# Where the transfers that clear two scratch arrays are begun: spread over the slots, or three in a row behind the maxima

## The chip, the core and the metric

The kernel runs on one core of a Trainium2 chip. Its engines are TensorE (PE; its weight loads are shown apart as PEld), VectorE (DVE), ScalarE (ACT), GpSimd (POOL) and SyncE (SP), which computes nothing here and begins most of the transfers. The metric is the time of one execution on the device in microseconds, as the median of several runs. A profile is one execution with every instruction recorded; times inside it are counted from the start of its span.

## What is computed

The input `x` is 16 sequences of 256 tokens of 128 numbers. Cut to what matters:

```python
x = x + layernorm(attn0(layernorm(x)))            # causal, 16 heads of 8
h = layernorm(x)                                  # then a block of two layers on h
for l in range(2):
    h = h + attn(ln1(h), ...)                     # causal, 16 heads of 8
    g = ln2(h)
    h = h + (token_moe if l == 0 else seq_moe)(g) # 8 experts, the two best used
x = x + layernorm(h)
```

In the token layer every token goes through its own two experts of eight (128 to 512 to 128, GELU between); in the sequence layer a whole sequence goes through two experts, chosen from the mean of its tokens. So there are three attention stages of 16 sequences each, with a stage of experts behind the second and another behind the third.

## The kernel before

**Slots.** The order of all work is written out by hand. A `Plan` collects steps as (slot, phase, function); within a slot the phases are EARLY, MAIN and LATE, and equal ones keep the order in which they were put. Every engine gets its instructions in that order and works through them in order. A sequence's attention takes NT = 6 slots, and sequence i of the 48 starts at slot s0 = 6 i; `plan.shift` moves the third attention behind the token experts.

**Attention of one sequence** (`plan_sequence`). Scores are computed twice. `scores_max` (matmuls L276 and L299) runs LEAD = 10 slots ahead and DVE takes the maximum of every row (`mx`, L302). PE transposes the maxima (`transpose_max`, L493), ACT and DVE split them into a high and a low part (`mhi`, `mlo`), and SP sends these with two small transfers into rows 62 and 63 of `qk_rows` (L508), in slot 6 k + 3, phase EARLY. `scores_exp` (L276 and L320, from slot s0) reads them: a matmul then subtracts the maxima, and ACT takes the exponential (`pT`, L324). `weighted` (L339) multiplies by the values. Then `evict` and `compact` (L522, L523), `inverse` (L527, L528), `spread` (L534: `r`), `divide` (`y`, L541, on POOL) and `project_out` (`po`, L546). PSUM holds one bank pair `s1` for the maxima and one, `s2`, for the exponentials: the next maxima's matmuls wait until `mx` has been read.

**A pair of sequences** (`plan_pair`, once in 12 slots) is normed, transposed and projected; ACT and DVE write the result in a high and a low part (`hl`, L410 and L415), and SP copies it into `qk_rows` with eight transfers (`place`, L424) of 256 KB each: two late in slot s0 - 15, two early in the next, and four more two and three slots after the first. In the other six slots of the pair there are none of these.

**Behind the first attention** (`attention_0`, `after`): SP fetches `x` again as the residual (`xr`, L116), POOL adds it (`an`, L636), SP stores the sum (L637), and DVE and POOL norm it (`st_z`, `mv_z`, `rs_z`, `z`).

**The two scratch arrays.** The token experts work on tiles of 256 tokens of one expert. `x_rows` takes the tokens, scattered by POOL with indirect transfers (L883, after the layer's gate); its places that no token takes have to hold zeros. `y_rows` takes the results (L1176), from which `plan_combine` gathers two rows for each token (L756). Both are cleared beforehand from the tile `zeros`, with 88 transfers of 256 KB by SP: 68 for `x_rows`, 20 for `y_rows` (L1307). The n-th is put into slot 2 n.

**The token experts** (`plan_tokens`, in two parts of NA_T = 13 and 26 tiles). Each tile is fetched, transposed, taken through `plan_expert` (L1079, L1083, L1093), biased by DVE (`y_t`, L1172) and stored by POOL (L1176), five slots after its start. The first of the third attention's gathers (`plan_combine`, slot S_B + 2 NB_T + 2, LATE) fall among the last of these; NB_T is 14. The order between stores and gathers is set by hand: a list of the stores so far is handed to the first gather as its dependencies.

SP's transfers are given eight semaphores in turn, so that one also waits until the eighth before it has landed.

Of the kernel before, what the change touches and what calls it, by code (L numbers as in the profile page):

```python
# [18 lines left out]
B, T, D = 16, 256, 128  # L19
# [22 lines left out]
BA = 10  # L42
NB = B * T // TR
NTILE = 2 * B * T // TR + E - 1
NA_T = -(-(2 * BA * T - E * (TR - 1)) // TR)
NB_T = (2 * BA * T + E * (TR - 1)) // TR - NA_T
# [29 lines left out]
def sandwich_kernel(  # L76
# [13 lines left out]
    nc = tc.nc  # L90
# [100 lines left out]
    zeros = work.tile([P, 4 * D], F32, tag="w1", name="zeros", bufs=3)  # L191
# [68 lines left out]
    def transposed(srcs, tag, bank="m"):  # L260

        pt = ps_m.tile([P, 4, P], F32, tag=bank, name=f"pt_{tag}", bufs=2 if bank == "m" else 1)
        for i, src in enumerate(srcs):
            nc.tensor.transpose(pt[:, i], src, ident)
        return pt[:, 0 : len(srcs)].rearrange("p i t -> p (i t)")
# [82 lines left out]
    LEAD = 10  # L348
    NT = len(TILES)
    EARLY, MAIN, LATE = 0, 1, 2  # L350
# [270 lines left out]
    def attention_0(plan):  # L621
        def after(plan, s, b, po):
            st = {}

            def bias():
                st["x"] = load_x(b, "xr", 2)
                st["ao"] = work.tile([P, 2, D], F32, tag="ao", name=f"ao_{b}")
                bo = row[:, R_BOUT : R_BOUT + D].unsqueeze(1).to_broadcast([P, 2, D])
                nc.vector.tensor_tensor(st["ao"], po(), bo, ALU.add)

            def an():
                st["an"] = work.tile([P, 2, D], F32, tag="an", name=f"an_{b}")
                return st["an"]

            def residual():
                nc.gpsimd.tensor_tensor(st["an"], st["x"], st["an"], ALU.add)  # L636
                nc.sync.dma_start(x1_dram[b], st["an"])  # L637

            plan.put(s, bias)
            plan_norm(plan, s + 1, lambda: st["ao"], an, f"a{b}")  # L640
            plan.put(s + 3, residual)
            plan_norm(plan, s + 4, lambda: st["an"], lambda: z[b], f"z{b}")

        for g in range(B // 2):
            def source(k, g=g):
                return x0[2 * g + k]

            plan_pair(plan, 2 * g, 0, source, None, lambda dst, pt: nc.scalar.copy(dst, pt))
            for b in (2 * g, 2 * g + 1):
                if b + 4 < B:  # L650
                    def load(b=b):
                        x0[b + 4] = load_x(b + 4, "x0", 6)

                    plan.put(NT * 2 * g - 26 + 2 * (b % 2), load)
                plan_sequence(plan, b, 0, b, f"0_{b}", after)
# [92 lines left out]
    def plan_combine(plan, s, b, pace, adds):  # L748


        st = {}

        def gather(i):
            if i == 0:
                st["y"] = work.tile([P, 4, D], F32, tag="yg", name=f"yg_{b}")
            get = nc.gpsimd.indirect_dma_start(  # L756
                st["y"][:, i], None, y_rows,
                bass.IndirectOffsetOnAxis(ap=ix_y[:, 2 * b + i // 2, i % 2 : i % 2 + 1], axis=0),
            ).ins

            if i == 0 and b in (0, BA):
                for store in stores[: NA_T + NB_T] if b == 0 else stores[NA_T + NB_T :]:
                    tc.add_manual_dep(get, store.name, SYNC)
            apart_from(get, "y")

        def add(i):
            zt = z[b][:, i // 2]
            nc.vector.scalar_tensor_tensor(
                zt, st["y"][:, i], w_tok2[:, 2 * b + i // 2, i % 2 : i % 2 + 1], zt,
                ALU.mult, ALU.add,  # L770
            )

        for i in range(4):
            plan.put(s + i // pace, lambda i=i: gather(i))
            plan.put(adds[i // 2], lambda i=i: add(i))
# [34 lines left out]
    puts, stores, seen = [], [], [0]  # L810
# [15 lines left out]
    def apart_from(ins, group):  # L826

        tc.declare_no_dep(ins, group=group, reason="distinct rows")
        tc.add_to_no_dep_group(group, ins)
        nc.gpsimd.memset(apart, 0.0)  # L830
# [283 lines left out]
    def plan_tokens(plan, s, q):  # L1114

        x_blocks = x_rows.rearrange("(c i p) d -> c p i d", i=2, p=P)
        y_blocks = y_rows.rearrange("(c i p) d -> c p i d", i=2, p=P)
        spare = {}

        def room(m):  # L1120


            if m == 2:
                parts = work.tile([P, 8, 2, D], F32, tag="hl", name="x_hl", bufs=1)
                spare.update({2 + i: parts[:, i] for i in range(8)})
            if m == 10:
                parts = work.tile([P, 4, D], F32, tag="yg", name="x_yg")
                spare.update({m + i: parts[:, 2 * i : 2 * i + 2] for i in range(2)})
            if m == 12:
                spare[m] = work.tile([P, 4, D], F32, tag="xn", name="x_xn", bufs=1)[:, 0:2]  # L1130
            return spare.get(m)

        def unit(m):
            tag = f"t{q}_{m}"

            st = {}

            def fetch():
                if q:
                    load()  # L1140
                return nc.sync.value_load(ix_tile[q][0:1, m, 0:1], min_val=0, max_val=E - 1)

            def load():
                eng = nc.sync if q else nc.gpsimd
                c = eng.value_load(ix_tile[q][0:1, m, 1:2], min_val=0, max_val=BLOCKS - 1)
                st["xt"] = room(m) if q == 0 else None
                if st["xt"] is None:
                    st["xt"] = work.tile([P, 2, D], F32, tag="xr", name=f"xt_{tag}", bufs=2)
                get = eng.dma_start(st["xt"], x_blocks[bass.ds(c, 1)].squeeze(0)).ins
                for put in puts[seen[0] :]:  # L1150
                    tc.add_manual_dep(get, put.name, SYNC)
                seen[0] = len(puts)

            if q == 0:
                plan.put(s - 5 + m // 2, load, MAIN)

            def turn():

                st["pt"] = transposed(
                    [st["xt"][:, i] for i in range(2)], tag, "p" if q == 0 or m < NB_T else "m"  # L1160
                )

            def affine():
                st["h"] = work.tile([P, T], F32, tag="r", name=f"ht_{tag}")
                nc.scalar.activation(  # L1165
                    st["h"], st["pt"], AF.Identity,
                    bias=vec[:, C_LN2B : C_LN2B + 1], scale=vec[:, C_LN2W : C_LN2W + 1],
                )

            def done(po, b2):  # L1170
                y = work.tile([P, 2, D], F32, tag="ao", name=f"y_{tag}")
                nc.vector.tensor_tensor(y, po, b2.unsqueeze(1).to_broadcast([P, 2, D]), ALU.add)  # L1172
                st["y"] = y

            def store():
                store = nc.gpsimd.dma_start(y_blocks[NA_T * q + m], st["y"]).ins  # L1176
                stores.append(store)
                apart_from(store, "y")

            plan_expert(plan, s + 2 * m, tag, w_tok, fetch, lambda: st["h"], done)  # L1180
            plan.put(s + 2 * m + 5, store, EARLY)
            plan.put(s + 2 * m - 1, turn, MAIN)
            plan.put(s + 2 * m, affine, EARLY)

        for m in range(TILES_OF[q]):
            unit(m)
# [112 lines left out]
    plan = Plan()  # L1299
    start_steps(plan)  # L1300
    attention_0(plan)

    n = 0
    for t in (x_rows, y_rows):
        fill = t.rearrange("(c p r) d -> c p (r d)", p=P, r=4)
        for c in range(fill.shape[0]):
            plan.put(2 * n, lambda fill=fill, c=c: nc.sync.dma_start(fill[c], zeros))  # L1307
            n += 1
    layer_attention(plan, 0, B, finish_tok)

# [77 lines left out]
```

## Time and profile before

| | us |
|---|---|
| median of 3 runs (lowest, highest) | 1020.77 (1017.8, 1027.81) |
| the profiled execution, as timed | 1017.52 |
| its span in the profile | 1015.5 |
| PE busy | 923.1 (91%) |
| DVE, POOL, ACT busy | 674.6, 610.9, 568.0 |
| first and last clearing of `x_rows` begun at | 43.6, 350.7 |
| first and last clearing of `y_rows` begun at | 353.1, 440.8 |
| second attention ends, token experts run alone until about | 480, 640 |

The profiled execution is among the fast ones: 3.25 us under the median. A line of the waits is read as "who L-line <- what ended its idle time: us in total, times, longest us". In a timeline a line is: start, duration, engine and line, operation, output and inputs, count, and in brackets the idle time before it with what ended it. Idle time of an engine costs time only if the engine, or what waits for it, sets the end. For transfers begun by SP the profile has the time at which SP begins them, not that at which they land.

### The profile page before, as it was taken

To read this page: it belongs to the slowest core of one execution; us is meant where nothing else is said; L and a number is where in the kernel's file an instruction comes from. 1 tells how busy PE (TensorE), PEld (TensorE's weight loads), DVE (VectorE), ACT (ScalarE), POOL (GpSimd) and SP (SyncE) were. 2 spreads that over 40 slices of the span, in tenths; PEclk is the share of its full clock that TensorE was granted. 3 is DMA by queue.
4 is the path that set the end of the run, shared out by engine and by line. 5 is a ranking of instruction groups with operands and counts; after the bars stand their busy time and mean duration, and the time that the engine had idled before them with its cause. 6 is when DMAs were issued, how large, how long until landed. Compare 5 with 4: busy or idle time off the path is not lost. (4 is left out here: it accounts for less than half of the span.)

```text
span 1015.5 us, 29356 instructions
## 1 busy us (share of the span) xinstructions
PE 923.1 (91%) x11148; PEld 721.6 (71%) x11148; DVE 674.6 (66%) x1614; ACT 568.0 (56%) x903; POOL 610.9 (60%) x1028
## 2 busy tenths in 40 slices
PE   3799889999999999998889999889999999999996
PEld 1566666666667777775788898766676677689996
DVE  3668778888788888885433413468899988445433
ACT  3565556666566666565344555345666666754442
POOL 7114666667766477658675127658688643366655
PEclk8799999999999999998799999899999999999999
DMA  6657677777877765542656787935565556256773
GB/s 162 136 121 174 169 179 188 182 188 192 191 178 173 170 168 155 166 132 71 198 166 190 218 235 235 242 91 119 125 128 116 106 113 144 67 151 197 203 202 106
DMA packets 143900, 163.64 MB, mean 161 GB/s; under 512 B 26928, under 2 KB 109872, under 8 KB 143760
## 3 DMA queue, kind: packets, MB, share of 16 engines
q1 hardware_dynamic: 133920, 142.41, 57.2%
q0 software_dynamic: 7312, 17.18, 5.6%
q10 hardware_dynamic: 2528, 2.18, 1.0%
q8 instruction: 88, 1.44, 0.6%
q14 instruction: 52, 0.43, 0.1%
HBM read 65.38 MB, written 37.36 MB: 101 GB/s over the span
## 5 line engine op out<-in xcount | busy, mean ns | idle before, releaser
L302 DVE TENSOR_REDUCE mx<-s 128x4 f32<-128x1024 f32 (+1 forms) x288 | 350.6, 1218 | 94.2 <-PE s L299 89.8
L324 ACT ACTIVATE pT<-s 128x1024 f32<-128x1024 f32 x288 | 294.4, 1023 | 164.4 <-PE s L320 160.3
L276 PEld LDWEIGHTS <-pick 64*128 64x128 bf16 x2304 | 78.1, 95 | 144.6 <-issue 122.1
L299 PE MATMUL s<-qk_rows 62*128 62x128 f32 (+1 forms) x1536 | 160.4, 306 | 11.0 <-DMA qk_rows<-hl 11.0
L320 PE MATMUL s<-qk_rows 64*128 64x128 f32 (+1 forms) x1536 | 158.4, 305 | 9.1 <-DMA qk_rows<-mlo 9.1
L339 PE MATMUL av<-pT,va 128*32 128x256 f32 (+1 forms) x3072 | 156.3, 333 | 0.0
L299 PEld LDWEIGHTS s<-qk_rows 62*128 62x128 f32 x1536 | 114.2, 194 | 13.6 <-issue 11.6
L320 PEld LDWEIGHTS s<-qk_rows 64*128 64x128 f32 x1536 | 112.3, 193 | 12.9 <-DMA qk_rows<-mhi 11.6
L276 PE MATMUL s<-mask_q,pick 64*128 64x128 bf16 (+1 forms) x1152 | 95.0, 243 | 18.8 <-DVE mx L302 14.5
L1083 ACT ACTIVATE gs_t<-ph_t,w_t 128x256 f32<-128x256 f32 x156 | 65.3, 470 | 71.5 <-PE ph_t L1079 67.0
L276 PE MATMUL s<-mask_k,pick 64*128 64x128 bf16 (+1 forms) x1152 | 94.2, 242 | 11.6 <-ACT pT L324 9.4
L339 PEld LDWEIGHTS av<-pT,va 128*32 128x32 f32 x3072 | 79.7, 110 | 33.3 <-issue 1.1
L1083 ACT ACTIVATE gs_s<-ph_s,w_s 128x256 f32<-128x256 f32 x128 | 52.7, 470 | 59.4 <-issue 57.3
L1093 PE MATMUL pe_t<-w_t,gs_t 128*128 128x128 f32 x624 | 80.4, 284 | 2.1 <-DVE y_t L1172 2.1
L1079 PE MATMUL ph_t<-ht_t,w_t 128*128 128x256 f32 x312 | 79.2, 398 | 1.7 <-ACT ht_t L1165 1.2
L883 POOL DMA_INDIRECT x_rows<-zn,ix_tok x64 | 65.1, 1017 | 25.5 <-issue 14.8
L1093 PEld LDWEIGHTS pe_t<-w_t,gs_t 128*128 128x128 f32 x624 | 76.2, 199 | 3.5 <-DVE y_t L1172 2.6
L756 POOL DMA_INDIRECT yg<-y_rows,ix_y x64 | 64.3, 1004 | 13.0 <-issue 12.7
L1172 DVE TENSOR_TENSOR y_t<-pe_t,w_t 128x256 f32<-128x256 f32 x39 | 16.5, 422 | 81.0 <-PE pe_t L1093 72.7
L1079 PEld LDWEIGHTS ph_t<-ht_t,w_t 128*128 128x128 f32 x312 | 58.7, 199 | 10.9 <-DVE mx L302 1.6
L1176 POOL DMA_DIRECT2D y_rows<-y_t x39 | 28.9, 742 | 60.6 <-DVE y_t L1172 48.4
L1093 PE MATMUL pe_s<-w_s,gs_s 128*128 128x128 f32 x512 | 62.8, 276 | 0.6 <-issue 0.6
(205 smaller groups left out, 1505.8 us busy)
## 6 DMA issues: line engine op xcount, KB each, us to landing
qk_rows<-hl SPq DMA_DIRECT2D x188, 256.0 KB
x_rows<-zeros SPq DMA_DIRECT2D x68, 256.0 KB
w_t<-in_w_tok SPq DMA_DIRECT2D x39, 320.0 KB
w_s<-in_w_seq SPq DMA_DIRECT2D x32, 320.0 KB
w_t<-in_w_tok SPq DMA_DIRECT2D x39, 258.0 KB
w_s<-in_w_seq SPq DMA_DIRECT2D x32, 258.0 KB
y<-at SPq DMA_DIRECT2D x48, 128.0 KB
r<-inv SPq DMA_DIRECT2D x96, 64.0 KB
```

The lines of the kernel that those rows point to most:

```text
L276: nc.tensor.matmul(s[:, a, :, o + 64 * c : o + 64 * c + 64], pick[h, c], masks[m][h, 0:nj], start=(c == 0), stop=False, skip_group_check=True,
L299: nc.tensor.matmul(s[:, a, j], qs, ks, start=False, stop=(j == nj - 1), skip_group_check=True)
L302: nc.vector.tensor_reduce(mx[:, 0 if u is None else 1, :, j0 : j0 + nj], s, AX.X, ALU.max)
L320: nc.tensor.matmul(s[:, a, j], ks, qs, start=False, stop=(j == nj - 1), skip_group_check=True)
L324: nc.scalar.activation(pT, sc, AF.Exp, scale=SCALE)
L339: nc.tensor.matmul(o[:, P:] if u is None else o, v[:, i, 8 * par + 4 * a + jj % 4], p[:, a, j], start=(c not in first), stop=False, skip_g ...
L756: get = nc.gpsimd.indirect_dma_start(st["y"][:, i], None, y_rows, bass.IndirectOffsetOnAxis(ap=ix_y[:, 2 * b + i // 2, i % 2 : i % 2 + 1], ...
L883: put = nc.gpsimd.indirect_dma_start(x_rows, bass.IndirectOffsetOnAxis(ap=ix_tok[:, 4 * g + i, k : k + 1], axis=0), zns[2 * g + i // 2][:, ...
L1079: nc.tensor.matmul(p, w1[:, f * P : (f + 1) * P], h_of(), start=True, stop=True)
L1083: nc.scalar.activation(st["gs"][:, f], p, AF.Gelu, bias=b1[:, f : f + 1])
L1093: nc.tensor.matmul(po[:, i] if last is None else st["po"][i][:, 0], st["gs"][:, f, i * P : (i + 1) * P], st["w2"][0][:, f], start=(f == 0) ...
L1176: store = nc.gpsimd.dma_start(y_blocks[NA_T * q + m], st["y"]).ins
```

## The change

The clearing transfers are put into slots 3, 4 and 5 of every six, three in a row from the slot in which the maxima are sent, phase LATE, in place of every second slot. Beside that, the store of one tile of results (number 13 of the second part) goes one slot earlier, by which it comes ahead of the first two gathers, and two assertions state how many stores and scatters have been put in order at that time.

```diff
@@ plan_combine
             if i == 0 and b in (0, BA):
+                assert len(stores) >= (NA_T + NB_T if b == 0 else NTILE)
                 for store in stores[: NA_T + NB_T] if b == 0 else stores[NA_T + NB_T :]:
                     tc.add_manual_dep(get, store.name, SYNC)
@@ plan_tokens
                 get = eng.dma_start(st["xt"], x_blocks[bass.ds(c, 1)].squeeze(0)).ins
+                if m == 0:
+                    assert len(puts) == (4 * B if q else 4 * BA)
                 for put in puts[seen[0] :]:
@@
-            plan.put(s + 2 * m + 5, store, EARLY)
+            plan.put(s + 2 * m + (4 if q and m == NB_T - 1 else 5), store, EARLY)
@@ sandwich_kernel
     n = 0
     for t in (x_rows, y_rows):
         fill = t.rearrange("(c p r) d -> c p (r d)", p=P, r=4)
         for c in range(fill.shape[0]):
-            plan.put(2 * n, lambda fill=fill, c=c: nc.sync.dma_start(fill[c], zeros))
+            slot = NT * (n // 3) + (NT - LEAD + 1) % NT + n % 3
+            plan.put(slot, lambda fill=fill, c=c: nc.sync.dma_start(fill[c], zeros))
             n += 1
```

## Prediction

> **What bounds the kernel now.** I read the page's busy table first: PE is busy 923.1 of 1015.5 us, DVE 66%, ACT 56%, POOL 60%. The chain that ended last names almost nothing (PE 8%), so the end is set by PE's order and the gaps in it. The fills (the transfers that clear `x_rows` and `y_rows`) are issued from 43.6 to 440.8 us; what they can cost is idle time of PE in that stretch. So the second view is the waits between 40 and 310 us, one line a releaser (total us, times, longest us), from the answers for PE, POOL and DVE:
>
> ```profile
> PE s L320 <- DMA qk_rows<-mlo: 9.1, 10, 1.8
> ...
> PE po L546 <- POOL y L541: 2.2, 5, 0.5
> ...
> POOL an L636 <- DMA xr<-in_x: 28.4, 8, 4.2
> ...
> DVE st_z L237 <- POOL an L636: 12.7, 8, 2.2
> ```
>
> Ten times PE waits for the maxima rows (`mlo`, L508), 9.1 us in all: that is what the change addresses. The third line matters as much: eight times POOL waits for `xr`, the residual input that SP fetches behind the `hl` rows. The third view is the timeline of one of these stretches, SP's queue first (start, us, line, operation):
>
> ```profile
> 204.73 2.62 SPq L424 DMA_DIRECT2D qk_rows<-hl  x4
> 207.45 0.60 SPq L528 DMA_DIRECT2D inv<-sums  x1
> 208.10 0.95 SPq L1307 DMA_DIRECT2D x_rows<-zeros  x1
> 209.15 2.82 SPq L424 DMA_DIRECT2D qk_rows<-hl  x4
> 212.01 1.01 SPq L116 DMA_DIRECT2D xr<-in_x  x1
> ...
> 218.15 0.34 SPq L1307 DMA_DIRECT2D x_rows<-zeros  x1
> 219.06 0.57 SPq L508 DMA_DIRECT2D qk_rows<-mhi  x1
> 219.73 0.54 SPq L508 DMA_DIRECT2D qk_rows<-mlo  x1
> ```
>
> Eight `hl` transfers of 256 KB come in a burst once per pair of sequences (12 slots, about 27 us). The windows show it (columns: stretch, PE, PEld, DVE, ACT, POOL, clock, DMA share, GB/s):
>
> ```profile
> 206.00:211.00 5.00, 4.88 (x85) 4.05 (x84) 3.96 (x9) 2.83 (x5) 4.16 (x7) 1.00 1.10 209
> 211.00:212.50 1.50, 1.50 (x28) 0.79 (x26) 1.22 (x2) 1.00 (x2) 0.00 (x0) 1.00 1.10 314
> 212.50:217.00 4.50, 4.35 (x74) 3.33 (x73) 4.14 (x12) 3.52 (x6) 2.52 (x4) 1.00 1.15 197
> ```
>
> The DMA engines are full from 206 to 217 us and `hl` runs at about 200 GB/s. What is queued at 212 waits until 217. POOL, DVE and PE then show what follows from that, in the same stretch:
>
> ```profile
> 219.40 0.73 POOL L636 TENSOR_TENSOR an<-xr,an 128x256 f32<-128x256 f32 x1 [3.28 <-DMA xr<-in_x]
> ...
> 222.78 0.73 POOL L541 TENSOR_TENSOR y<-y,r 128x256 f32<-128x256 f32 x1
> ```
>
> ```profile
> 220.16 0.29 DVE L237 BATCH_NORM_STATS2 st_z<-an 128x6 f32<-128x128 f32 x1 [1.32 <-POOL an L636]
> ...
> 221.23 1.16 DVE L302 TENSOR_REDUCE mx<-s 128x8 f32<-128x1024 f32 x1
> ```
>
> ```profile
> 221.84 0.66 PE L320 MATMUL s<-qk_rows 64*128 64x128 f32 x8 [0.61 <-DMA qk_rows<-mlo]
> 222.45 0.29 PE L276 MATMUL s<-mask_q,pick 64*128 64x128 bf16 x4
> ...
> 223.56 0.71 PE L546 MATMUL po<-wvo_sb,y 128*128 128x128 f32 x4 [0.53 <-POOL y L541]
> ```
>
> `xr`, issued at 212.01, lets POOL start `an` at 219.40. From there POOL works without a gap to the end of `y` at 223.51, and PE's `po` starts 0.05 us later. DVE, held by `an`, ends `mx` at 222.39, and PE's L276 at 222.45 needs that bank. So the wait for the maxima (0.61 us) lies under a second chain, **xr, an, y or mx, PE**, which ends at the same moment. The engine that looks off the path is on it.
>
> **The change, part by part.**
>
> *The fills, order.* No instruction is added or removed; PE, ACT and DVE keep their order. Before, fill n is begun at slot 2n; after, at slots 3, 4 and 5 of every six, the maxima being sent early in slot 3. In the built program the burst becomes hl hl F hl hl inv F hl hl F hl hl xr, where it was hl x4, inv, F, hl x4, xr, with one fill ahead of it (served before 204 us, when the DMA was idle) and two behind `xr`. (In the last bursts, planned by `layer_attention`, the first of the three stands ahead of the first `hl`; the count is the same.) No bytes are added, but **two more fills stand between the first `hl` and `xr`**.
>
> *Cost of a fill in the burst.* Upper end: 262,144 bytes at some 345 GB/s, the rate of the fullest half microseconds while a fill is served, 0.75 us. Lower end: the burst moves 8 x 262 KB of `hl` in the 11.0 us from 206 to 217; at 197 GB/s that alone takes 10.6, so the one fill in it took 0.4. I take 0.55, between the two, since both are of the same burst: two fills 1.1 us (0.8 to 1.5).
> The Trainium skill's page "DMA: Bandwidth & Descriptors", section "Anatomy of one DMA — SWDGE (gpsimd) path", prices a transfer at about 2.0 us plus its bytes over 436 GB/s. By it `xr` (128 KB, issued at 212.0) would land by about 214.3, before POOL has finished the instruction ahead of `an` (at 216.11), and two fills issued earlier would cost nothing. The row says 7.4 us from issue to `an`: the fit is for one transfer alone, on the other queue, and here the queue is the price. I follow the row; with the page's bytes term a fill would be 0.60 us, two 1.2.
>
> *What PE pays.* `xr` lands 1.1 later, `an` and so `y` end 1.1 later. For the six stretches at 169, 197, 224, 250, 277 and 305 us `po` follows `y` within 0.1 us: 6 x 1.1 = 6.6. At 142 `y` ends at 142.71 and `po` starts at 142.84: 1.0. At 114 `y` ends at 113.48 and `po` starts at 113.90, so 0.7. Sum **+8.3 us** (5.5 to 11.5).
>
> *The maxima.* A transfer of SP also waits for the eighth before it. Before, `mlo` is issued at 219.73, behind `mhi` and a fill that waited for the seventh `hl` to land (218.1). After, the eighth before `mlo` is that seventh `hl` (in the stretches at 113 and 142 the eighth one), itself two fills later: 218.1 + 1.1 = 219.2. The maxima come about 0.5 us earlier, not more: the fill that left their front now stands in front of what they wait for. Under the xr chain this gives PE nothing in eight places. It counts at 84.20 (wait of 0.62, no `xr` there, `y` ended 2.6 before `po`): -0.4. The wait at 42.68 (1.65) has no fill ahead of it and stays. If the xr chain were not there, the most to be had is 9.1 - 1.65 = 7.4.
>
> *First maxima of the next pair.* PE needs the first four `hl` at 212.60; they now land one fill later (0.55). The trace shows no wait there; the slack lies between 0 and about 1.7 us (fourth `hl` issued at 206.74 and its bytes through by about 211). A wait of up to 0.55 falls ahead of the 1.1 + 1.1 us that PE idles later in the stretch, and is taken out of it: 0 (at most 8 x 0.55 = 4.4 if nothing absorbs it).
>
> *After 310 us* there is no `xr`, no wait for maxima, and `hl` issued from 338.18 is first used at 347.37, with its first four transfers through by about 344.5: 0; up to 0.5 in each of 7 bursts if that cover is thinner. The fill that ends `x_rows` moves two slots (4.6 us), to about 355; POOL's first scatter is at 359.0: 0, at most 1 us once. `y_rows` is filled 180 us before its use: 0. In the other half of each pair the DMA is lightly loaded: 0.
>
> *The store of tile 13 of the second part* (`NB_T - 1`) moves up one slot, ahead of the first two gathers of `plan_combine`, on POOL:
>
> ```profile
> 613.68 0.76 POOL L1176 DMA_DIRECT2D y_rows<-y_t  x1 [0.31 <-DVE y_t L1172]
> ...
> 614.74 0.99 POOL L756 DMA_INDIRECT yg<-y_rows,ix_y  x1 [0.23 <-issue]
> ```
>
> Before, two gathers (610.96 and 612.30) fill the time in which POOL would wait for `y_t`; after, POOL idles from 610.7 to 613.68, the store goes, and all four gathers of z[0] follow from 614.74. Everything behind is 2 x 1.28 = 2.6 us late. DVE's additions (620.77) wait for the fourth gather: 618.54 + 3.5 (median landing) = 622.0. POOL's `rs_i` (623.66) comes at 626.2, DVE's `xn` (624.79) at 627.3, and behind `xn` on DVE stands `y_t`, which frees PE's bank for the matmul at 625.91: now about 628.3. **+2.3 us**; ends 0.5 (POOL catches up) and 4.
> Does the gather also wait until the store has landed (3.4 us, median of that row)? The same page, "Two DMAs through the same engine are not ordered", says that only the completion semaphore orders them, which would put the gather at 617.1 and the sum 2.4 higher. The trace has gathers 0.26 us behind a store (609.94, 610.96), and in the changed program's list the first gather has no wait on that store's lane: I take none.
>
> **Sum.** 8.3 - 0.4 + 2.3 = +10.2 us. The profiled execution took 1017.52 (span 1015.5): 1027.7. The median of the runs shown is 1020.77, 3.25 above it, from which it would be 1031.0. I give 1029, between them. Own range 1023 to 1037.
>
> **Rivals.**
> *A, the maxima decide (faster).* If the two fills do not delay `xr` (they overlap with `hl`[...]: for it speaks the 0.4 end above), the 7.4 us of waits for maxima go, less what `y` and `mx` still hold; with the store's 2.3 against it, 1017.5 - 7.4 + 2.3 = 1012. It decides once a fill in the burst costs less than some 0.1 us. Against it: the DMA share is 1.10 to 1.15 in the burst, and `y` ends 0.05 before `po`.
> *B, no visible change.* The delay of `xr` and the gain of the maxima cancel, or later slack gives it back, and the store costs 0 to 3: 1018 to 1023, say 1020.
> *C, more is lost.* A fill costs its full 0.75, the first maxima wait as well, or the gather waits for the store: 11.5 + 4 + 2 = 1035.
>
> **How the numbers follow.** Forecast 0.50, A 0.14, B 0.24, C 0.12. About 1% (10 us) is what a measurement of this kernel can tell from no change. The forecast lies right at it: half of it counts as slower. Slower by over 1%: 0.26 + 0.11 and, since what I have costed at nothing can only add, 0.07 more: 0.44. Faster by over 1%: the lower half of A, 0.08. Within: 0.48. The range leaves out most of A and the end of C: 1015 to 1037.
>
> **What would show it.** Right: POOL's wait for `xr` grows from 28.4 by about 9 us over eight times; PE's wait for `mlo` falls to about 4 or less; PE's waits for `y` (L546) and for `mx` (L276) grow by about 8 together; between 610 and 635 us PE has about 2.3 us more idle time. Wrong: POOL's wait for `xr` stays at 28, or PE's waits for `mlo` go and nothing takes their place.

## The result, and the profile after

The changed kernel takes 1028.6 us (median of 13 runs, 1022.45 to 1038.1) against 1020.77 (13 runs, 1014.89 to 1027.81) for the kernel before: **1.0082 times, 95% interval 1.0058 to 1.0106**, or 5.9 to 10.8 us more. The ratios, and the mean clocks of runs below, leave out runs that took over 1.5% longer than the fastest of their kernel. The forecast of 1029 is met to half a microsecond. That is partly luck. From the median of before, the forecast's own sum of 10.2 us leads to 1031.0; it was set 2 us lower, between two bases, and the fills cost less than the sum said. The profiled execution took 1028.54 (span 1026.6), 11.0 more than the one before: near the 10.2, but with a loss of clock in it that the sum had no term for.

First the waits between 40 and 320 us in the kernel after (total us, times, longest us), the stretch in which fills and `xr` meet:

```profile
POOL an L636 <- DMA xr<-in_x: 35.6, 8, 5.1
DVE st_z L237 <- POOL an L636: 14.9, 8, 3.1
...
PE s L276 <- DVE mx L302: 8.7, 17, 1.5
...
PE po L546 <- POOL y L541: 4.0, 8, 0.5
PE s L299 <- DMA qk_rows<-hl: 3.9, 5, 1.0
PE s L320 <- DMA qk_rows<-mlo: 3.4, 3, 1.5
```

The wait for the maxima rows (`mlo`) fell from 9.1 to 3.4 us. In its place stand POOL's wait for `xr` (28.4 to 35.6), DVE's for `an` (12.7 to 14.9), and on PE the waits for `mx` (1.8 to 8.7) and `y` (2.2 to 4.0). One line is new: the first maxima wait for `hl` (3.9 us, five times). The cure of one wait is paid for in another, as forecast. The timeline of the stretch that the prediction showed (start, us, line, operation, idle time before it), SP first:

```profile
209.40 1.28 SPq L424 DMA_DIRECT2D qk_rows<-hl  x2
210.73 0.61 SPq L1312 DMA_DIRECT2D x_rows<-zeros  x1
...
213.68 0.84 SPq L1312 DMA_DIRECT2D x_rows<-zeros  x1
214.62 2.10 SPq L424 DMA_DIRECT2D qk_rows<-hl  x2
216.77 0.61 SPq L1312 DMA_DIRECT2D x_rows<-zeros  x1
217.42 1.22 SPq L424 DMA_DIRECT2D qk_rows<-hl  x2
218.68 0.97 SPq L116 DMA_DIRECT2D xr<-in_x  x1
```

```profile
224.51 0.73 POOL L636 TENSOR_TENSOR an<-xr,an 128x256 f32<-128x256 f32 x1 [3.73 <-DMA xr<-in_x]
...
227.90 0.73 POOL L541 TENSOR_TENSOR y<-y,r 128x256 f32<-128x256 f32 x1
```

```profile
227.57 0.29 PE L276 MATMUL s<-mask_q,pick 64*128 64x128 bf16 x4 [0.25 <-DVE mx L302]
...
228.68 0.71 PE L546 MATMUL po<-wvo_sb,y 128*128 128x128 f32 x4 [0.53 <-POOL y L541]
```

Three fills stand ahead of `xr`, POOL starts `an` 15.11 us after the burst's first `hl` (224.51 - 209.40), and `po` follows the end of `y` (228.63) by 0.05 us. No wait for `mlo` is left in this stretch. Before, the same distance was 219.40 - 204.73 = 14.67. So the two fills cost 0.44 in this stretch of this pair of executions, not the 1.1 of the sum.

The store of tile 13 did what was forecast. The matmul of PE that needs the bank freed by `y_t`, in the kernel after:

```profile
637.29 3.52 PE L1094 MATMUL pe_t<-w_t,gs_t 128*128 128x128 f32 x16 [2.28 <-DVE y_t L1175]
```

Before, no matmul waits for `y_t` there; the forecast was 2.3.

PE's projections (`po`, L546) are good milestones, 48 in each execution. Their times after less those before are: -0.45 at 85 us, +0.8 at 114, +1.8 at 143, **+3.6 at 156, +4.4 at 170**, +4.7 at 197, +5.1 at 224, +6.1 at 250, +7.3 at 277, +7.8 at 305, +9.3 at 318, then +9.0 to +9.3 from 344 to 482, and +10.7 to +11.0 from 723 on. The loss ends with the first attention, as forecast. But it doesn't come in equal steps of 1.1. At 156 and 318 us it jumps, where no `xr` is waited for. For the first jump the windows tell why (stretch, busy us of PE, PEld, DVE, ACT, POOL, granted clock, DMA share, GB/s). Before, from 85 to 155 us:

```profile
85.00:155.00 70.00, 64.52 (x956) 46.68 (x955) 56.40 (x114) 40.87 (x53) 43.12 (x69) 0.98 0.71 176
```

and after:

```profile
85.00:155.00 70.00, 64.74 (x888) 45.62 (x887) 52.87 (x107) 38.08 (x50) 40.72 (x64) 0.90 0.62 159
```

The granted TensorE clock was 0.90 instead of 0.98 in these 70 us. PE looks as busy as before and does 7% fewer matmuls. The prediction has no term for that. At 310 to 320 us, ahead of the second jump, 1.75 us of full clock are lost, and PE waits once for 1.8 us until ACT has written `pT`.

### The profile page after: what moved, and what is told of

It reads as the page before. It is cut to its first block, busy times and chain, and to the rows that moved or that the text cites. A ratio compares the mean times of both kernels' runs of the same rounds, so it can differ in the third digit from the quotient of the medians.

```text
span 1026.6 us, 29367 instructions
## 1 busy us (share of the span) xinstructions
PE 926.0 (90%) x11148; PEld 722.9 (70%) x11148; DVE 675.6 (66%) x1614; ACT 569.1 (55%) x903; POOL 613.2 (60%) x1028
## 5 line engine op out<-in xcount | busy, mean ns | idle before, releaser
L299 PE MATMUL s<-qk_rows 62*128 62x128 f32 (+1 forms) x1536 | 161.1, 307 | 14.9 <-DMA qk_rows<-hl 14.9
L339 PE MATMUL av<-pT,va 128*32 128x256 f32 (+1 forms) x3072 | 158.9, 337 | 0.0
L299 PEld LDWEIGHTS s<-qk_rows 62*128 62x128 f32 x1536 | 114.9, 195 | 19.2 <-issue 17.3
L276 PE MATMUL s<-mask_k,pick 64*128 64x128 bf16 (+1 forms) x1152 | 94.2, 242 | 12.0 <-ACT pT L324 10.7
L1175 DVE TENSOR_TENSOR y_t<-pe_t,w_t 128x256 f32<-128x256 f32 x39 | 16.5, 423 | 78.3 <-PE pe_t L1094 69.9
```

What stands on the lines that cost most here:

```text
L276: nc.tensor.matmul(s[:, a, :, o + 64 * c : o + 64 * c + 64], pick[h, c], masks[m][h, 0:nj], start=(c == 0), stop=False, skip_group_check=True,
L299: nc.tensor.matmul(s[:, a, j], qs, ks, start=False, stop=(j == nj - 1), skip_group_check=True)
L339: nc.tensor.matmul(o[:, P:] if u is None else o, v[:, i, 8 * par + 4 * a + jj % 4], p[:, a, j], start=(c not in first), stop=False, skip_g ...
```

## The experiments

The theories, as the expectations name them. **T1**: two more fills ahead of `xr` delay `an`, and with it `y`, `mx` and PE. **T2**: the late `hl` transfers, and the first maxima that wait for them (L299), carry the loss. **T3**: the store's wait is absorbed before the end. **T4**: only how many fills fall into the busy stretch counts. **Gate theory**: stalls that follow each other closely make the granted clock drop to half for some 3.4 us, and this is a part of every loss.

The runs were made on other chips than the first result. There the kernel before takes 1060 to 1068 us: the first 370 us are as fast as on the first chip (the projection at 358.76 comes at 357.50 in store_only, whose order is that of before up to there), the excess lies behind, where the change moves only the one store. So each ratio is against the kernel before on the same chip. The table also gives the time between the projections that stand at 85 and 359 us in the profile before, and the full clock lost between them: the sum over 5 us windows of 5 x (1 - granted clock).

| kernel | time against before (95%) | us from projection to projection | clock lost, us | the same at equal clock |
|---|---|---|---|---|
| before | 1 | 273.3 | 3.4 | 270.9 |
| before_again | | 279.1 | 12.0 | 270.6 |
| store_only | 1.0014 (0.9989 to 1.0039) | 273.3 | 3.4 | 270.8 |
| after | 1.0082 (1.0058 to 1.0106) | 282.8 | 8.4 | 276.8 |
| after_again | 1.0117 (1.0076 to 1.0157) | 286.8 | 15.4 | 275.9 |
| fills_only | 1.0040 (1.0013 to 1.0067) | 278.6 | 4.7 | 275.3 |
| fills_445 | 1.0103 (1.0070 to 1.0136) | 286.1 | 11.9 | 277.7 |
| fills_heavy | 1.0318 (1.0275 to 1.0361) | 309.1 | 30.7 | 287.3 |
| heavy_warm | 1.0345 (1.0303 to 1.0387) | 305.5 | 20.6 | 290.9 |
| fills_012 | 0.9883 (0.9827 to 0.9938) | 274.2 | 6.9 | 269.3 |
| fills_light | 0.9958 (0.9929 to 0.9987) | 272.1 | 5.1 | 268.5 |
| before_xr | 0.9983 (0.9957 to 1.0009) | 274.9 | 10.3 | 267.6 |
| fills_xr | 0.9883 (0.9843 to 0.9924) | 264.8 | 0.0 | 264.8 |
| light_xr | **0.9853** (0.9812 to 0.9893) | 259.8 | 0.0 | 259.8 |

The last column takes off 0.71 us for each us of clock lost. That slope is fitted to six executions: three with the fills of before (before, before_again, store_only) and three with those of after (after, after_again, fills_only), a level for each group and one slope for both. It is a fit to few points, and for fills_heavy and heavy_warm it is carried far beyond them.

**The two parts alone** (store_only, fills_only).

```diff
-            plan.put(s + 2 * m + 5, store, EARLY)
+            plan.put(s + 2 * m + (4 if q and m == NB_T - 1 else 5), store, EARLY)
```

> Before, with only the store of tile 13's tokens moved one gather place earlier (ahead of the first two gathers of the combine), the fills as in before. T1 and T2 (both treat the store as a separate step): the store begins its wait before the first two gathers, both gathers and so rs_i, xn and y_t come about 2.3 us later, a matmul of pe_t waits about 2.3 us for y_t, and the end comes 2.0 to 2.6 us later: about +2.3 us. Rival T3 (the wait is absorbed again before the end of the kernel): 0 to +0.5 us.

By time the store is worth -1.2 to +4.1 us, which doesn't tell 2.3 from nothing. The row does. The first fence is store_only, the second fills_only, where the store is at its old place:

```profile
650.69 2.64 PE L1093 MATMUL pe_t<-w_t,gs_t 128*128 128x128 f32 x16 [2.70 <-DVE y_t L1172]
```

```profile
650.41 2.05 PE L1093 MATMUL pe_t<-w_t,gs_t 128*128 128x128 f32 x16 [0.55 <-DVE y_t L1174]
```

The wait is 2.70 us with the store moved and 0.55 without: some 2.1 us go with the store. On the first chip PE's projections are 8.3 and 9.1 us late ahead of it (494 and 508 us) and 10.7 behind it (723 us), so 1.6 to 2.5 more. The rows speak against T3; by time it stays open.

```diff
-            plan.put(2 * n, lambda fill=fill, c=c: nc.sync.dma_start(fill[c], zeros))
+            slot = NT * (n // 3) + (NT - LEAD + 1) % NT + n % 3
+            plan.put(slot, lambda fill=fill, c=c: nc.sync.dma_start(fill[c], zeros))
```

> The fills as in after (slots 3, 4 and 5 of every six), the store of tile 13 at its place of before. T1 and T2: the whole loss of the fills' region, about +9 us less the 0.4 that comes back later, so +6 to +9 us against before by the chain, about +6 by the medians (after is +7.8 by its median, less 2.3 for the store). The wait for y_t in front of pe_t is back at its value of before. If the store carried the loss in another way than by that wait, this run is within 2 us of before.

+4.2 us (1.4 to 7.1): the fills are the larger part, but they cost less than the 8.3 of the sum, and less than the 6 to 9 expected here.

**xr taken out of the burst** (before_xr: with the fills of before; fills_xr: with those of after).

```diff
@@ attention_0, after
+            def residual_load():
+                st["x"] = load_x(b, "xr", 2)
+
+            plan.put(s - NT, residual_load)
             def bias():
-                st["x"] = load_x(b, "xr", 2)
```

> Before, with the fetch of xr issued six slots earlier, ahead of the burst of maxima rather than in it. T1 (xr behind the burst sets when an, st_z, mx and y come): POOL's an no longer waits for xr, PE's waits for y and mx fall to those of slots outside the burst; 1 to 4 us below before, since the wait for mlo at L320 remains. T2 (the late maxima transfers hl are what delay PE; xr is slack): within 1 us of before.

> The fills as in after, the store as in before, and xr fetched six slots earlier, so that three fills still stand in the burst but none ahead of xr. T1 (the two further fills cost what they delay xr by): the loss of the fills goes, 0 to 5 us below before, POOL's wait for xr about 0; the first maxima's waits at L299 (3.9 us in five places in after) remain or grow a little. T2 (the late hl transfers and what follows them carry the loss): +4 to +8 us against before, with the waits at L299 as large as in after or larger.

fills_xr is 12.4 us faster than before (8.1 to 16.7): with `xr` out of the way the three fills in the burst cost nothing. T2, which asked for +4 to +8, falls; T1 has the sign, but its gain of 0 to 5 us was too small. 8.5 us of the gain lie in the stretch of the table, 6.0 at equal clock. before_xr gains less: POOL waits no longer for `xr`, and yet only 1.8 us are gained (between a gain of 4.6 and a loss of 0.9). That is within T1's 1 to 4, but the interval doesn't rule out T2's "within 1 us". PE's waits for the maxima from 40 to 320 us in before_xr:

```profile
PE s L320 <- DMA qk_rows<-mlo: 7.8, 9, 1.5
```

Of PE's 9.1 us of waits for the maxima rows 7.8 are left. The fills of before stand ahead of these, and they end where the chain of `xr` ended. Of two chains that end together, taking one away gives little.

**Where the fills stand** (fills_445: slots 4, 4, 5 of six, the first four `hl` ahead of them; fills_012: slots 0, 1, 2; fills_light: slots 3 to 7 of twelve, none in the burst; light_xr: the same with the early `xr`). Only the line of the slot differs:

```diff
+            slot = NT * (n // 3) + (4, 4, 5)[n % 3]                     # fills_445
+            slot = NT * (n // 3 + 1) + n % 3                            # fills_012
+            slot = 2 * NT * (n // 6) + (3, 3, 4, 5, 6, 7)[n % 6]        # fills_light, light_xr
```

> The fills three in a row as in after, but begun half a slot to a slot later (slots 4, 4, 5 of every six, each behind the maxima of its slot), so that in the burst the first four hl transfers go out ahead of all fills, and all three fills still go ahead of xr; the store as in before. T1 (what counts is that two more fills stand ahead of xr): as with the fills alone, +3 to +7 us against before, the waits for xr at 33 to 36 us in the stretch 40 to 320, the waits for hl at L299 down from 5.2 us to under 2. T2 (the late first maxima, hl at L299, carry the loss): the waits for hl go and with them most of the loss, -1 to +2 us.

The waits for `hl` are gone, and the kernel is slower than with the fills alone. The lines are PE's and POOL's waits from 40 to 320 us in fills_445:

```profile
PE s L276 <- ACT pT L324: 10.9, 12, 2.0
PE s L276 <- DVE mx L302: 9.2, 17, 1.2
...
PE s L299 <- DMA qk_rows<-hl: 0.4, 1, 0.4
```

```profile
POOL an L636 <- DMA xr<-in_x: 35.2, 8, 5.6
```

T2 falls a second time. T1 has the sign and the wait for `xr`, but its +3 to +7 is too small against 7.4 to 14.5: in the 300 us of the table 7.3 us more of clock were lost than in fills_only (5.2 by the slope), and 2.4 us more at equal clock. For these the waits show a path that no theory had: PE's wait for `pT` doubled, from 5.2 us in fills_only to 10.9. The tile `hl` exists only once (`bufs=1` in the code), so ACT can write the next `hl` (L410), and behind it `pT`, only when the eight transfers have read the last one. What delays them delays ACT; fills_heavy below shows it most clearly.

> The fills three in a row in slots 0, 1 and 2 of every six: none of them ahead of xr in the burst, but three around and behind it, where before has one or two, and so ahead of mhi and mlo; the store as in before. T1 (xr's place in the queue): xr lands about 0.5 us sooner than in before, so POOL's waits for xr fall from 28 us to about 24, while mlo comes later and PE's waits for it at L320 rise from 9 us to 12 to 16: the sum is 0 to +4 us against before. Rival T4 (only how many fills fall into the busy stretch counts, not which transfer they delay): as with the fills alone, +3 to +7 us, with the waits for xr no shorter than in before.

The waits for `xr` fell to 24.5 us as T1 said, so T4 falls. PE's waits for `mlo` stayed at 9.8 us where 12 to 16 were expected. The time is 1.2% lower than before, below either range. In the 300 us of the table only 1.5 of that is found at equal clock; where the rest comes from is open. Behind its projection at 375 us the profiled execution of fills_012 takes 680 us; those of before_again, store_only, before_xr and fills_only, also on other chips than the first, take between 681 and 691 there.

> All six fills of a pair of sequences in its light half (slots 3 to 7 of every twelve), none in the burst's slots 9 to 12; the store as in before. T1: xr waits for no fill, mhi and mlo neither: POOL's waits for xr fall from 28 us to 22 to 25, PE's waits for mlo and mhi from 9 and 12 us to under 4 each: -3 to -9 us against before. T2 says the same sign by the hl transfers, but only -1 to -3 us, since in before they are hardly waited for.

4.5 us faster (1.4 to 7.5): right in sign and size. The waits for `mlo` and `mhi` fell to 1.5 and 1.8 us, those for `xr` only to 26.8, since `xr` still stands behind eight `hl`. (The profiled execution, whose waits these are, took 1066.32 us, 8 more than the median of this kernel.)

> The fills in the light half as in the run beside it, and xr fetched six slots earlier, ahead of the burst. T1 (xr and then mlo are what is waited for in the burst): no wait for xr is left, mlo and mhi wait for no fill: -10 to -15 us against before, at most 3 us better than the fills as in after with the early xr (which gave -12.4), since that had only the waits for hl at L299 left. Gate theory (stalls of 2 to 3 us one after the other make the granted clock drop to half for a window of some 3.4 us, and this is a part of every loss): the mean granted clock of the runs is 0.955 or more, against 0.947 in before, and the stretch from 80 to 320 us shows at most one stretch below 0.9. T2: within 3 us of the fills in the light half alone.

15.6 us faster (11.4 to 20), the best of all kernels here and a little more than the 10 to 15 expected. Neither chain is left, and each alone had given only 1.8 and 4.5. The first of its windows (the third column from the end is the granted clock):

```profile
85.00:155.00 70.00, 66.83 (x1009) 48.21 (x1006) 58.69 (x121) 43.59 (x56) 46.00 (x73) 1.00 0.82 189
```

The clock is full here and in the windows that follow up to 320 us. The mean clock of its runs is 0.954 at the median against 0.948, a hair under the 0.955 expected.

**What the clock is worth** (the two kernels unchanged, once more).

> The kernel after, once more, beside another execution of the kernel before. Between about 70 and 373 us the first profiles differ by 9.5 us (place of the projection at 85 against that at 372), and the granted clock cost after 8.6 us of full clock there against 3.4 in before. Gate theory (short stalls in a row make the clock drop to half for some 3.4 us, in windows that fall differently in each execution): the differences in these 300 us change from one pair of executions to the next with the lost clock, by about 0.6 us for each us lost, and what is left without it is 5 to 7 us in both pairs. Rival (the clock is only a mark of the waits): the difference stays 9 to 10 us whatever the lost clock. Over the whole kernel: +5 to +9 us, since the fills alone gave +4.2 and the store 1.5 by time and about 2.2 by its wait for y_t.

> The kernel before, once more, as the other half of the pair: waits for xr at 28 to 29 us and for mlo at about 9 us in the stretch 40 to 320, as in its first profile; one to three windows of half clock between 70 and 375 us, not at the same places.

By time the kernel after is 12.5 us slower in this pair (8.1 to 16.8), above the 5 to 9 expected but for the edge. The strongest row is that of the kernel before against itself. Its second profile, from 85 to 210 us:

```profile
85.00:155.00 70.00, 64.26 (x884) 46.06 (x884) 53.16 (x109) 38.25 (x49) 39.39 (x63) 0.90 0.67 165
155.00:210.00 55.00, 51.90 (x721) 36.76 (x714) 41.28 (x82) 30.50 (x40) 33.11 (x52) 0.91 0.72 171
```

The waits are those of the first profile (27.9 us for `xr`, 8.8 for `mlo`), the instructions the same, and the same 300 us take 5.8 us longer with 8.6 us more of clock lost, in four places where one to three were expected. One instruction shows it too. `po` of the fifth sequence, at half clock in after, and at full clock in fills_only, which has the same order up to there:

```profile
144.66 1.22 PE L546 MATMUL po<-wvo_sb,y 128*128 128x128 f32 x4 [0.19 <-POOL y L541]
```

```profile
143.91 0.71 PE L546 MATMUL po<-wvo_sb,y 128*128 128x128 f32 x4 [0.53 <-POOL y L541]
```

This is the jump of +1.8 between 143 and 156 us: fills_only loses nothing there. The first pair (after less before) differs by 9.5 us with 5.0 us more of clock lost, the second by 7.7 with 3.4. Taking off 0.71 a microsecond leaves 5.9 and 5.3, within the 5 to 7 expected, where the rival had the difference stay at 9 to 10. A third pair, fills_only less store_only, differs by 5.3 with 1.3 more: 4.4 are left. So the difference does move with the clock lost; three pairs don't give the size of what is left to better than a microsecond. Over 52 whole runs of before on one chip, too, the time goes up by 0.45 us for each us of clock lost (correlation 0.80).

The Trainium skill's page "TensorE: Matmul & The Clock Gate", section "Part 1: The HAM clock gate (the "warmup" mystery)", says that an idle window of about 3.4 us halves the clock, and that these windows run freely and don't start with the kernel. The traces agree in the length: a drop costs about 1.7 us of full clock (1.75 at 110 to 120 us in before) or twice that (3.4 at 140 to 150 us in after), which is 3.4 or 6.8 us at half. They agree in that the same program drops at other places in another execution. They don't show the idle window: no single wait of PE from 40 to 320 us is longer than 2.8 us in any run here, and from 140 to 144 us in after, ahead of and at the start of a drop, PE was busy in 1.71 of the 4 us. That PE's waits trip it is seen here only as company: this drop comes amid waits of 0.85 us (for `mlo`, until 141.60) and 1.28 us (for `mx`, until 143.54).

**More of the cause** (fills_heavy: all six fills ahead of `xr`; heavy_warm: with extra matmuls of zero weights).

```diff
+            slot = 2 * NT * (n // 6) + (9, 10, 10, 10, 11, 11)[n % 6]
```

> All six fills of a pair in slots 9 to 11 of every twelve, so that six instead of one stand ahead of xr in the burst (five more than before, where after has two more); the store as in before. T1 with the forecast's price (0.55 us a fill, 8 bursts that count): 5 x 0.55 x 8 = +22 us, the longest wait for xr 6.5 to 8 us. T1 with the price of the profiles (two fills moved POOL's an by 0.44 us in the stretch at 210 us, so 0.22 a fill): +9 us, and 2 to 5 more by the clock: +11 to +14, the longest wait for xr about 5.5. T2 (first maxima): the waits for hl at L299 grow from 5.2 to 15 us or more.

+34.7 us by the medians (29 to 39 by the interval), more than any theory had. `an` starts 17.65 us after the first `hl` on average, against 15.0 in before and 15.8 in after; the longest wait for `xr`, 6.6 us, is as T1 with the forecast's price had it. At equal clock five fills cost 287.3 - 270.8 = 16.5 us in the 300 us, 0.41 for each fill and stretch; the clock lost, 30.7 us against 3.4, is worth 19 if the slope holds so far out. T2 falls once more: the waits for `hl` at L299 are 0.5 us. But most of what PE newly waits for isn't T1's chain either. PE's waits for `y` and `mx` from 40 to 320 us are 10.8 us (4.0 in before), those for `pT` 19.5 (4.4 in before), one of 1.8 to 2.8 us in each of eight bursts. ACT and then PE, at 208 us:

```profile
208.36 0.69 ACT L410 ACTIVATE hl<-pp,vec 128x512 fp32r<-128x512 f32 x1 [3.17 <-DMA r<-inv]
```

```profile
210.01 0.40 PE L276 MATMUL s<-mask_k,pick 64*128 64x256 bf16 x4 [2.02 <-ACT pT L324]
```

This is the path of the single `hl` tile. ACT starts 0.23 us before POOL's `an` (208.59), since `xr` stands right behind the last `hl`. (The trace infers the releaser, and names `r`; the matmul that ACT needs was done at 206.) In after this path is hardly longer than in before (5.7 us against 4.4), so that the chain of `xr` is what the change lengthened. No run here gives `hl` a second tile.

> All six fills in slots 9 to 11 of every twelve, as in the run with 1.0318, and in the eighth slot-11 step of each pair of the first layer (ahead of PE's longest stall, 2.0 us in the stretch at 208 us) the twelve matmuls of `av` once more with zero weights, which add nothing to `av` but keep PE busy about 1.1 us longer. PE's order is otherwise the same; what waits for DMAs waits for them as before. Gate theory (a window of low PE activity makes the clock drop, and the dropped clock, not only the waits, costs time): the full clock lost between 70 and 375 us falls from 30.7 us to 10 to 20, and the kernel comes out 5 to 11 us under the run without the extra matmuls, at 1.021 to 1.027 of before. Rival (the lost clock is only a mark of the stalls): the same time as without them or up to 3 us more, 1.030 to 1.035. If the lost clock does not fall, the run tells nothing between the two.

```diff
             for k in (n, n + 1):
                 weighted(k, b, st["p", k], st["av"], first)
+            if n == 2 and i < B and i % 2:
+                for k in (n, n + 1):
+                    weighted(k, b, st["p", k], st["av"], first, True)   # zero weights
```

By its time, 1.0345, this run lies where the rival put it (1.030 to 1.035), and not where the gate theory did. It still doesn't decide between them, because the extra matmuls were put into the wrong slots, as heavy_warm's own timeline of PE shows:

```profile
191.41 1.05 PE L339 MATMUL av<-pT,zeros 128*32 128x256 f32 x24
...
206.21 0.39 PE L276 MATMUL s<-mask_k,pick 64*128 64x256 bf16 x4 [1.16 <-ACT pT L324]
```

They stand 15 us ahead of the stall they were to fill, where PE had other work, and add 1.05 us to it in each pair. The lost clock fell to 20.6 us and the time of the whole kernel didn't, but with 8 us of work added neither theory can be read from it. That filling the stalls keeps the clock up is not shown.

## Why the prediction was right, and where it was not

**The mechanism** (`xr`, `an`, `y` or `mx`, PE): right. The named waits grew (POOL's for `xr` by 7.2 where about 9 was said, PE's for `y` and `mx` by 8.7 where about 8 was said), that for `mlo` fell below 4, and with `xr` out of the burst the loss is gone. The delays show on PE: its waits from 40 to 320 us add up to 17.5 us in before and 25.7 in after, 8.2 more, where the sum had 7.9.

**The price of two fills** (1.1 us, 0.8 to 1.5): too high. From the first `hl` of a burst to `an` the eight stretches take 15.0 us on average in before (15.1 in its second profile) and 15.8 in both profiles of after: 0.8, or 0.5 in fills_only. A fill delays what stands behind it by less than its 0.55. The fills' part of the sum, 8.3 - 0.4, measured 5.2 at equal clock, and 4.2 (1.4 to 7.1) by the time of fills_only. The lower end of 5.5 was nearest. Why PE's waits grew by more than the time is not shown.

**The clock**: missing. The sum took each wait at its length. In the pair of first profiles 5.0 us more of full clock were lost in after, worth 3.6 us by the slope (2.4 in the second pair). This made up for the term above, so that the pair's 11.0 came out near the sum's 10.2. The medians don't need it: 5.2 for the fills and 2.3 for the store are 7.5, and they differ by 7.8. There the sum was 2.4 us too high, and the forecast was right because its base was chosen 2 us low. Whether the change itself makes the clock worse is open: over whole runs fills_only lost 54.7 us of clock on average and before, on the same chip, 54.1 (standard errors 1.6 and 0.9); after_again lost 62.9 and before beside it 58.0 (1.9 and 1.7).

**The maxima half a microsecond earlier**: consistent with the wait for `mlo` that fell, and with the burst in which it is gone. **First maxima of the next pair at 0**: they do wait (3.9 us in after, 0.9 in its second profile), but the kernel in which they don't is slower. **After 310 us nothing**: right, apart from the drop of the clock and the wait for `pT` at 310 to 320 us in after. **The store +2.3**: right by the row (waits of 2.28, 2.74 and 2.70 us in three profiles; 0.55 in fills_only without the move), within a wide interval by time. The gathers followed the store by 1.0 us and didn't wait until it had landed.

**Rivals.** A (the maxima decide, faster) fails on the chain of `xr`; it is what happens once `xr` is gone, as fills_xr shows. B (no visible change) and C (1035) lie outside the interval's 1026.7 to 1031.6 (1020.77 times its ends).

## What to carry to other kernels

When two transfers that are both waited for stand in one queue, moving fillers from one to the other only changes the name of the wait; look at which transfers must come soon, and take those out of the burst (here by an earlier fetch of data that was long ready), and the fillers too. Two chains that end together have to be shortened together: 1.8 and 4.5 us alone became 15.6. A delayed burst also holds the tile it reads from, and with it the engine that wants to write there next. And read the granted clock by windows before waits are added up, and never from one execution alone: a difference of a few microseconds between two profiles can be the clock.

## What the runs showed of the hardware

The spread of this kernel from run to run is in good part the clock: two executions of the same program lost 3.4 and 12.0 us of full clock in the same 300 us, and took 273.3 and 279.1 us. Each us of clock lost cost 0.71 us there by a fit to six executions, and 0.45 us over 52 whole runs. The clock fell to half without any wait of PE longer than 2.8 us. A 256 KB fill in a full queue delayed what stood behind it by 0.2 us (half of fills_only's 15.5 - 15.1 against store_only) to 0.5 us (a fifth of fills_heavy's 17.65 - 15.0), less than the 0.75 of the prediction's upper end.
